# A graph layer on one core: GpSimd's gathers with a one-column memset once in three batches, and their wait for TensorE two batches further back

## The chip, the cores and the metric

The kernel runs on one core of a Trainium2 chip. A core has five engines with an instruction stream each: TensorE (PE: matmuls, PEld: its weight loads), VectorE (DVE), ScalarE (ACT), GpSimd (POOL) and SyncE (SP, which only issues DMAs). They wait for each other through semaphores. The metric is the device time of one execution in microseconds (us).

## The reference

One layer of a graph network with 12500 nodes of 160 features (64 scalars and 32 vectors of 3), and 400000 edges, sorted by their destination. Cut to what matters here (some lines joined):

```
h = jnp.maximum(_layernorm(x, axis=-1), 0.0)     # x0, x1: 64 scalars and 32 vectors of h; a = node_vec1
y0 = x0 @ W_l1_0 * a * inv0
y1 = jnp.einsum('nuc,uv->nvc', x1, W_l1_1) * a[:, :, None] * inv1
w = silu(edge_attr_16 @ fc_W1 * (1.0 / math.sqrt(FC_IN))) @ fc_W2 * (1.0 / math.sqrt(FC_H))   # 192: w_a, w_b, w_c, w_d
ys0, ys1 = y0[edge_src], y1[edge_src]
e0, e1 = edge_attr[:, :1], edge_attr[:, 1:]
mid0 = concatenate([w_a * ys0 * e0, w_d * einsum('euc,ec->eu', ys1, e1) * (1.0 / math.sqrt(3.0))])
mid1 = concatenate([(w_b * ys0)[:, :, None] * e1[:, None, :], (w_c * e0)[:, :, None] * ys1])
z0 = jnp.zeros((n, MID), mid0.dtype).at[edge_dst].add(mid0) * inv_nb
z1 = jnp.zeros((n, MID, 3), mid1.dtype).at[edge_dst].add(mid1) * inv_nb
out = x + C_S * (h's scalars @ W_sc0, vectors @ W_sc1) * a + C_X * (z0 @ W_l2_0, z1 @ W_l2_1) * a   # scaled
```

Each edge reads the row of y (y0 and y1 side by side, 160 wide) of a random node. This read is what GpSimd does in the kernel.

## The kernel before, in words

A first stage of about 190 us (the loop's first gather starts at 192.7) computes the node rows y and writes them to DRAM (y_d). The rest is one loop over the edges. They stand in 3125 tiles of 128, four tiles (GT) to a batch: 782 batches (NB). For each batch b:

- load(b): GpSimd gathers the rows of the 4 tiles into one buffer yg (128 x 4 x 160), with one indirect DMA for each tile (L579). There are 11 such buffers (YB). 24 of the 782 batches are not gathered but "made": their rows are rebuilt on the other engines, into buffers of their own (every 24 batches at first, 17 of them, then every 42).
- weigh(b): PE makes the 192 weights of each edge by 4 matmuls (L609) into one of two PSUM buffers pw; ScalarE then copies three of the edge's numbers beside them (L611). lift_rows(b): ScalarE scales the rows into yge (L521, four times).
- dots_of(b) and products(b): VectorE forms the products pr (L526 and L528; L532, L533, L536 and L537, by these lines in this order). L532 is the last to read yg. Once in three batches it also builds the selection matrices sel for 12 tiles (L628).
- sums(b): PE adds the products up by destination, pz += sel.T @ pr (L648).

The order of the instructions on PE, ScalarE and VectorE is that of the code in one loop over b, written by hand (`manual_schedule`); the engines run freely along it and are tied only by semaphores. An iteration b does weigh(b + 2), lift_rows(b + 2), dots_of(b + 1), products(b + 1), load(b + AHEAD), sums(b), and small steps for finished groups. As there are two pw, the weigh of b + 2 waits for the products of b; these wait for L526 and L528, which wait for L611 of their batch, which waits for PE's signal that the matmuls of weigh are done.

GpSimd is not in the list of hand-ordered engines. Its gathers wait for three things: for the DMA queue's semaphores (eight gathers back), at the first gather of a batch for the buffer, that is for L532 and L521 of the batch that had it 11 gathered batches before (DVE and Activation in the rows below), and, at one gather of each batch, for PE: `weighed[b]` holds the name of the last weigh matmul of batch b, and load(b) ties its gather k == 0 to `weighed[b - AHEAD + 2]`, with AHEAD = 10.

Of the kernel before, what the change touches and what calls it, by code (L numbers as in the profile page):

```python
# [9 lines left out]
F32 = mybir.dt.float32  # L10
# [7 lines left out]
P = 128  # L18
# [12 lines left out]
TG = 12  # L31
EG = 8
YB = 11
AHEAD = 10
WIDE = 3, 5
GN = 8
HN = 2
# [9 lines left out]
def kernel(  # L47
# [19 lines left out]
    nc = tc.nc  # L67
# [44 lines left out]
    def made(b):  # L112

        return made_at.index(b) if b in made_at else None
# [173 lines left out]
    def load_xe(blk):  # L288

        if blk not in blocks:  # L290
            xe = ld.tile([P, 512], F32, name="xe")
            v = e16[blk * P:(blk + 1) * P, :].rearrange("(s k f) (h c) -> k s (f h) c", s=4, k=2, h=2)
            for k in range(2):
                nc.sync.dma_start(xe[:, 256 * k:256 * (k + 1)], v[k])
            blocks[blk] = xe

    def e4_load(q):

        if q * EG < NU and q not in raws:
            lo, hi = q * EG * TG, min((q + 1) * EG * TG, TP)  # L300
            raw = ld.tile([P, EG * TG, 4], F32, name="raw")
            nc.sync.dma_start(raw[:, :hi - lo, :].rearrange("p t c -> p (t c)"), e4[:, lo * 4:hi * 4])
            raws[q] = raw
# [26 lines left out]
    engines = {mybir.EngineType.PE, mybir.EngineType.Activation, mybir.EngineType.DVE}  # L330
# [179 lines left out]
    keep = ctx.enter_context(tc.tile_pool(name="keep", bufs=1))  # L510
# [30 lines left out]
    with (  # L541
# [9 lines left out]
        leaving, weighed = [], {}  # L551
# [13 lines left out]
        def first_of(b):  # L565
            return min(b * GT if b <= short else short * GT + (T - short * GT) // 2 if b < NB else T, T)

        def tiles_of(b):
            return list(range(first_of(b), first_of(b + 1)))

        def load(b):
            r = made(b)
            if r is not None:
                rows[b] = xms[r]
                return
            yg = ygp.tile([P, GT, D], F32, name="yg")
            rows[b] = yg
            for k, t in enumerate(tiles_of(b)):
                ins = nc.gpsimd.indirect_dma_start(  # L579
                    out=yg[:, k, :], out_offset=None, in_=y_d,  # L580
                    in_offset=bass.IndirectOffsetOnAxis(ap=src_sb[:, t:t + 1], axis=0))
                if k == 0 and b - AHEAD + 2 in weighed:
                    tc.add_manual_dep(ins.ins, weighed[b - AHEAD + 2], mybir.DependencyInfo(
                        mybir.DependencyClass.Sync, mybir.DependencyReason.DATA), reason="no further ahead of the weights")

# [37 lines left out]
        def select(u, pw):  # L623

            n = min(TG, T - u * TG)
            sels[u] = selp.tile([P, TG, WN], F32, name="sel")
            for_each = pw[:, :, SP:].unsqueeze(1).to_broadcast([P, n, GT, WN // GT])
            nc.vector.tensor_tensor(sels[u][:, 0:n, :].rearrange("p t (k c) -> p t k c", k=GT), for_each,  # L628
                                    drel[:, u * TG:u * TG + n].unsqueeze(2).unsqueeze(3).to_broadcast(
                                        [P, n, GT, WN // GT]), ALU.is_equal)  # L630

        def dots_of(b):
            tmp = part.tile([P, GT, 3, M1], F32, name="tmp")
            dot(tmp, wts[b], rows[b], len(tiles_of(b)))
# [158 lines left out]
            for f in todo:  # L793
                f()

        order = tc.manual_schedule(engines={mybir.EngineType.PE, mybir.EngineType.Activation, mybir.EngineType.DVE})
        with order:
            e4_load(0)
            for blk in range(min(AHEAD - 1, NB - 1) * GT // BT + 1):
                load_xe(blk)  # L800
            for b in range(min(AHEAD - 1, NB)):
                load(b)
# [11 lines left out]
            dots_of(0)  # L814
            if AHEAD - 1 < NB:
                load(AHEAD - 1)
            select(0, wts[0])
# [3 lines left out]
            for g, e in enumerate(last_batch):  # L821
                at_end = e + 4 >= NB
                t = e + (1 if at_end else 2)
# [5 lines left out]
            for b in range(NB + 3):  # L829
                u, k = divmod(b, K)  # L830
# [22 lines left out]
                if b + AHEAD < NB:  # L853
                    load(b + AHEAD)
# [150 lines left out]
```

## Time and profile before

| | |
|---|---|
| median of 3 runs | 4750.52 us (4744.84 to 4751.22) |
| profiled execution | 4710.4 us, span 4708.5 us |
| mean granted TensorE clock | 0.916 |
| busy: PE, DVE, POOL, ACT | 85%, 75%, 63%, 37% of the span |
| the gather L579 | 3029 times, 949 ns each |

The profile is one execution, 40 us shorter than the median. In a group's row stand the busy time, the mean of one, and the idle time of the engine just before such an instruction with what ended it: "issue" is a gap in which the engine waited for nothing that the profile shows, and "remote" is a wait whose releaser the profile could not find on this core. In a row of the timeline stand the start, the duration, the engine, the line, the operation, how often it is repeated on end, and in brackets the idle time before it.

### The profile page before, as it was taken

The numbers are of one execution on the slowest core, as the hardware profiler recorded it, in microseconds if no ns is written. First come the engines' busy times: TensorE is split into PE (matmuls) and PEld (weight loads), VectorE is DVE, ScalarE is ACT, GpSimd is POOL, SyncE is SP. The second block draws the span as 40 slices with busy tenths as digits, with TensorE's granted clock in tenths as the row PEclk, the third lists the DMA queues.
The fourth block names the chain that finished last, engine by engine and source line by source line (L and its number), as shares of the span: only waits on it lengthen the run. The fifth ranks groups of instructions, "written<-read, shape, count | busy, mean of one in ns | idle before, by whom it ended". The sixth has DMA issues, their size and how long they took to land. (4 is left out here: it accounts for less than half of the span.)

```text
span 4708.5 us, 55993 instructions
## 1 busy us (share of the span) xinstructions
PE 4005.0 (85%) x16409; PEld 2323.1 (49%) x16409; DVE 3520.9 (75%) x6817; ACT 1764.2 (37%) x5610; POOL 2970.4 (63%) x3132
## 2 busy tenths in 40 slices
PE   4578888888888888888888888988888888888888
PEld 4444554444545554444444444555455455555554
DVE  4467777777777777777777777777777777777777
ACT  4333333333333333333333333333333333333333
POOL 5566666666666666666666666666666666666663
PEclk8689999999999999999999988999999999989899
DMA  7422222222222222222222222222222222232222
GB/s 215 122 62 63 67 65 68 68 61 66 65 69 66 66 67 65 63 65 68 67 65 66 65 64 62 66 67 62 68 62 66 62 68 62 68 107 64 63 63 58
DMA packets 228622, 335.20 MB, mean 71 GB/s; under 512 B 55098, under 2 KB 171910, under 8 KB 228054
## 3 DMA queue, kind: packets, MB, share of 16 engines
q0 software_dynamic: 150000, 256.20, 22.2%
q1 hardware_dynamic: 64642, 67.02, 4.6%
q10 hardware_dynamic: 13668, 8.36, 0.6%
q8 instruction: 130, 2.13, 0.2%
q14 instruction: 182, 1.49, 0.1%
HBM read 307.49 MB, written 23.88 MB: 70 GB/s over the span
## 5 line engine op out<-in xcount | busy, mean ns | idle before, releaser
L579 POOL DMA_INDIRECT yg<-y_d,src_sb x3029 | 2874.5, 949 | 1610.9 <-issue 711.1
L648 PE MATMUL pz<-pr,sel 128*128 128x384 f32 x6250 | 2488.7, 546 | 32.0 <-issue 16.3
L648 PEld LDWEIGHTS pz<-pr,sel 128*128 128x128 f32 x6250 | 1249.1, 210 | 979.0 <-issue 429.0
L609 PE MATMUL pw<-w,hT 64*128 64x192 f32 x6250 | 810.7, 366 | 553.4 <-issue 295.7
L611 ACT ACTIVATE pw<-raw 128x12 f32<-128x12 f32 (+1 forms) x782 | 140.4, 180 | 2812.0 <-remote 1339.0
L521 ACT ACTIVATE yge<-yg,raw 128x160 f32<-128x160 f32 x3029 | 1042.0, 422 | 0.3 <-DMA yg<-y_d,src_sb 0.3
L609 PEld LDWEIGHTS pw<-w,hT 64*128 64x128 f32 x6250 | 538.6, 195 | 944.7 <-issue 545.7
L526 DVE TENSOR_TENSOR tmp<-yg,pw 128x384 f32<-128x384 f32 (+1 forms) x758 | 416.6, 550 | 561.3 <-ACT pw L611 534.9
L533 DVE TENSOR_TENSOR pr<-pr,pw 128x768 f32<-128x768 f32 (+1 forms) x782 | 745.2, 953 | 27.0
L528 DVE TENSOR_REDUCE yg<-tmp 128x128 f32<-128x384 f32 (+1 forms) x758 | 450.3, 594 | 403.0 <-ACT yge L521 348.3
L628 DVE TENSOR_TENSOR sel<-pw,drel 128x1536 f32<-128x1536 f32 (+1 forms) x261 | 455.3, 1744 | 0.0
L592 PE MATMUL px<-xe,w 32*128 32x512 f32 x782 | 439.4, 643 | 11.1 <-issue 8.6
L532 DVE TENSOR_TENSOR pr<-pw,yg 128x384 f32<-128x384 f32 (+1 forms) x758 | 420.2, 554 | 17.8
L537 DVE TENSOR_TENSOR pr<-pw,yge 128x384 f32<-128x384 f32 (+1 forms) x782 | 428.3, 548 | 0.0
L536 DVE TENSOR_TENSOR pr<-pw,yge 128x256 f32<-128x256 f32 (+1 forms) x782 | 326.4, 417 | 0.0
L597 ACT ACTIVATE hT<-px 128x512 f32<-128x512 f32 x391 | 228.7, 585 | 12.4 <-issue 11.5
L592 PEld LDWEIGHTS px<-xe,w 32*128 32x128 f32 x782 | 114.7, 184 | 209.3 <-issue 142.9
L675 PEld LDWEIGHTS px<-wc,za 128*128 128x128 f32 x1110 | 151.3, 194 | 39.6 <-issue 7.6
L693 DVE SCALAR_TENSOR_TENSOR acc<-os,by,acc 128x160 f32 x370 | 144.2, 390 | 14.4 <-ACT os L680 1.1
L675 PE MATMUL px<-wc,za 128*128 128x96 f32 x1110 | 150.0, 272 | 0.8 <-ACT za L666 0.6
L376 POOL DMA_INDIRECT xr<-in_x,src_sb x88 | 87.2, 991 | 67.7 <-issue 27.8
L662 PEld LDWEIGHTS pz<-ident,zs 128*128 128x128 f32 x555 | 72.4, 141 | 58.1 <-issue 33.9
(126 smaller groups left out, 1683.1 us busy)
## 6 DMA issues: line engine op xcount, KB each, us to landing
yg<-y_d,src_sb POOLq DMA_INDIRECT x3029
xe<-in_e SPq DMA_DIRECT2D x196, 128.0 KB
xr_d<-xr SPq DMA_DIRECT2D x24, 320.5 KB
y_d<-ys ACTq DMA_DIRECT2D x12, 640.0 KB
xm<-xr_d SPq DMA_DIRECT2D x24, 320.0 KB
acc<-in_x SPq DMA_DIRECT2D x11, 640.0 KB
out<-acc SPq DMA_DIRECT2D x11, 640.0 KB
raw<-in_e SPq DMA_DIRECT2D x32, 192.0 KB
```

The lines of the kernel that those rows point to most:

```text
L521: nc.scalar.activation(yge[:, k, :], yg[:, k, :], AF.Copy, scale=e4v[:, k, 0:1])
L526: nc.vector.tensor_tensor(tmp[:, :n], y1, wt[:, :n, NW:NW + 3].unsqueeze(3).to_broadcast([P, n, 3, M1]), ALU.mult)
L528: nc.vector.tensor_reduce(yg[:, :n, M0:96], tmp[:, :n].rearrange("p t c u -> p t u c"), AX.X, ALU.add)
L532: nc.vector.tensor_mul(pr[:, :n, 0:96], wt[:, :n, 96:NW], yg[:, :n, 0:96])
L533: nc.vector.tensor_mul(pr[:, :n, 256:].rearrange("p t (c u) -> p t c u", c=3), pr[:, :n, 0:M0].unsqueeze(2).to_broadcast([P, n, 3, M0]), w ...
L536: nc.vector.tensor_mul(pr[:, :n, 96:160], wt[:, :n, 0:M0], yge[:, :n, 0:M0])
L537: nc.vector.tensor_mul(pr[:, :n, 160:256].rearrange("p t (c u) -> p t c u", c=3), wt[:, :n, M0:96].unsqueeze(2).to_broadcast([P, n, 3, M1] ...
L579: ins = nc.gpsimd.indirect_dma_start(out=yg[:, k, :], out_offset=None, in_=y_d, in_offset=bass.IndirectOffsetOnAxis(ap=src_sb[:, t:t + 1], ...
L592: nc.tensor.matmul(ph, w1[r, :], xe[r, :], start=True, stop=True)
L609: last = nc.tensor.matmul(pw[:, k, 0:NW], hids[s][r, o:o + P], w2[r, :], start=True, stop=True)
L628: nc.vector.tensor_tensor(sels[u][:, 0:n, :].rearrange("p t (k c) -> p t k c", k=GT), for_each, drel[:, u * TG:u * TG + n].unsqueeze(2).un ...
L648: nc.tensor.matmul(z_ps[g], sels[t // TG][:, t % TG, :], pr[:, k, M0:], start=first, stop=last)
```

## The change

Three edits. First, AHEAD goes from 10 to 12: load(b + 12) stands in iteration b, and the wait for PE in load(b) is for the weights of batch b - 10 instead of b - 8; it is tied to the last gather of the batch instead of k == 0. Second, once three batches have been passed since the last time, load(b) begins with a memset of one column of a small tile on GpSimd: 257 of them in all. Third, GpSimd joins the engines whose order is that of the code. The number of buffers stays 11.

```diff
-AHEAD = 10
+AHEAD = 12
+REST = 3
...
+        rest = keep.tile([P, 1], F32, name="rest")
+        rested = [0]
+
         def load(b):
             r = made(b)
+            rested[0] += 1
             if r is not None:
                 rows[b] = xms[r]
                 return
             yg = ygp.tile([P, GT, D], F32, name="yg")
             rows[b] = yg
-            for k, t in enumerate(tiles_of(b)):
+            if rested[0] >= REST and b >= AHEAD:
+                nc.gpsimd.memset(rest, 0.0)
+                rested[0] = 0
+            of = tiles_of(b)
+            for k, t in enumerate(of):
                 ins = nc.gpsimd.indirect_dma_start(
                     out=yg[:, k, :], out_offset=None, in_=y_d,
                     in_offset=bass.IndirectOffsetOnAxis(ap=src_sb[:, t:t + 1], axis=0))
-                if k == 0 and b - AHEAD + 2 in weighed:
+                if k == len(of) - 1 and b - AHEAD + 2 in weighed:
                     tc.add_manual_dep(ins.ins, weighed[b - AHEAD + 2], ...
...
-        order = tc.manual_schedule(engines={mybir.EngineType.PE, mybir.EngineType.Activation, mybir.EngineType.DVE})
+        order = tc.manual_schedule(engines={mybir.EngineType.PE, mybir.EngineType.Activation, mybir.EngineType.DVE,
+                                            mybir.EngineType.Pool})
```

GpSimd's instructions of before, from the middle of the program (each number behind yg is one batch's buffer; DMASW are the DMA queue's semaphores, PE the wait for weigh, DVE and Activation the wait for the buffer):

```order
1136 L579 DMA yg_11356<-y_d_60,src_sb_69 128x160 [waits DMASW3_49,PE_49]
1137 L579 DMA yg_11386<-y_d_60,src_sb_69 128x160 [waits DMASW4_49,DVE_49,Activation_49]
1138 L579 DMA yg_11386<-y_d_60,src_sb_69 128x160 [waits DMASW5_49]
1139 L579 DMA yg_11386<-y_d_60,src_sb_69 128x160 [waits DMASW6_49]
1140 L579 DMA yg_11386<-y_d_60,src_sb_69 128x160 [waits DMASW7_49,PE_49]
1141 L579 DMA yg_11425<-y_d_60,src_sb_69 128x160 [waits DMASW0_49,DVE_49,Activation_49]
```

The four gathers of yg_11386 stand with the buffer's wait on the first and PE's wait on the fourth: the scheduler has put k == 0 behind the other three.

The same after the change (L584 is the memset, L588 the gather; its Pool semaphore is that of the memset before):

```order
1182 L588 DMA yg_10995<-y_d_60,src_sb_69 128x160 [waits DMASW7_49,PE_49]
1183 L584 MEMSET rest_1704 128x1 [waits Pool_49]
1184 L588 DMA yg_11025<-y_d_60,src_sb_69 128x160 [waits DMASW0_49,DVE_49,Activation_49]
1185 L588 DMA yg_11025<-y_d_60,src_sb_69 128x160 [waits DMASW1_49]
1186 L588 DMA yg_11025<-y_d_60,src_sb_69 128x160 [waits DMASW2_49]
1187 L588 DMA yg_11025<-y_d_60,src_sb_69 128x160 [waits DMASW3_49,PE_49]
1188 L588 DMA yg_11065<-y_d_60,src_sb_69 128x160 [waits DMASW4_49,DVE_49,Activation_49]
```

The waits stand on the same places of a batch as before, buffer first and PE last; the value that PE's wait asks for is that of two batches earlier. New is the memset, which follows the last gather of one batch and stands ahead of the first of the next, as a rule once in 12 gathers. On PE, VectorE, ScalarE and SyncE the order is the same.

## The prediction

> **What bounds the kernel now.** I read the page's busy shares first, then the costliest groups, then the waits, and last a stretch of the timeline, because the first three leave open which engine makes the others late.
>
> ```profile
> PE 4005.0 (85%) x16409; PEld 2323.1 (49%) x16409; DVE 3520.9 (75%) x6817; ACT 1764.2 (37%) x5610; POOL 2970.4 (63%) x3132
> L579 POOL DMA_INDIRECT yg<-y_d,src_sb x3029 | 2874.5, 949 | 1610.9 <-issue 711.1
> L611 ACT ACTIVATE pw<-raw 128x12 f32<-128x12 f32 (+1 forms) x782 | 140.4, 180 | 2812.0 <-remote 1339.0
> L521 ACT ACTIVATE yge<-yg,raw 128x160 f32<-128x160 f32 x3029 | 1042.0, 422 | 0.3 <-DMA yg<-y_d,src_sb 0.3
> L526 DVE TENSOR_TENSOR tmp<-yg,pw 128x384 f32<-128x384 f32 (+1 forms) x758 | 416.6, 550 | 561.3 <-ACT pw L611 534.9
> ```
>
> TensorE (PE) has the largest share, but it is not full. Nobody waits for gathered rows: ScalarE lost 0.3 us to them in the whole run (third group). So Pool's gathers are not late. What is late is line 611, the small ScalarE copy that ends weigh: it starts when PE has reported its weigh matmuls, and VectorE's L526 starts behind it. There are 782 batches, and 758 of them are gathered, in 3029 gathers.
>
> ```profile
> ACT pw L611 <- remote: 1339.0, 196, 17.8
> ACT pw L611 <- PE pw L609: 712.1, 169, 9.3
> DVE tmp L526 <- ACT pw L611: 555.7, 236, 17.5
> POOL yg L579 <- issue: 711.1, 2304, 1.4
> POOL yg L579 <- remote: 449.8, 192, 4.0
> POOL yg L579 <- PE pw L609: 155.6, 75, 4.2
> ```
>
> The columns are total, times and longest, in us. Pool's own rests for a PE signal are the last two rows ("remote" is taken as the same wait with its releaser not found, for the stretch below shows the two alike): 192 + 75 = 267 rests, 449.8 + 155.6 = 605.4 us, 2.27 us each. One rest comes per 758 / 267 = 2.84 gathered batches. The other 2304 gaps are 0.31 us each (711.1 / 2304).
>
> ```profile
> 2053.49 0.95 POOL L579 DMA_INDIRECT yg<-y_d,src_sb  x1 [2.61 <-remote]
> 2058.33 0.92 PE L609 MATMUL pw<-w,hT 64*128 64x192 f32 x8 [1.44 <-DVE pr L537]
> 2059.35 0.18 ACT L611 ACTIVATE pw<-raw 128x12 f32<-128x12 f32 x1 [1.96 <-PE pw L609]
> ...
> 2062.93 0.92 PE L609 MATMUL pw<-w,hT 64*128 64x192 f32 x8
> ...
> 2067.27 0.94 POOL L579 DMA_INDIRECT yg<-y_d,src_sb  x1 [0.30 <-issue]
> ...
> 2070.68 0.18 ACT L611 ACTIVATE pw<-raw 128x12 f32<-128x12 f32 x1 [9.37 <-remote]
> 2070.87 0.94 POOL L579 DMA_INDIRECT yg<-y_d,src_sb  x1 [2.65 <-remote]
> 2070.90 0.55 DVE L526 TENSOR_TENSOR tmp<-yg,pw 128x384 f32<-128x384 f32 x1 [4.01 <-ACT pw L611]
> 2072.12 0.95 POOL L579 DMA_INDIRECT yg<-y_d,src_sb  x1 [0.30 <-ACT yge L521]
> 2073.47 0.56 DVE L532 TENSOR_TENSOR pr<-pw,yg 128x384 f32<-128x384 f32 x1
> ...
> 2079.68 0.95 POOL L579 DMA_INDIRECT yg<-y_d,src_sb  x1 [0.30 <-issue]
> 2080.69 0.92 PE L609 MATMUL pw<-w,hT 64*128 64x192 f32 x8
> 2082.49 0.18 ACT L611 ACTIVATE pw<-raw 128x12 f32<-128x12 f32 x1 [7.83 <-PE pw L609]
> 2082.68 0.95 POOL L579 DMA_INDIRECT yg<-y_d,src_sb  x1 [2.06 <-PE pw L609]
> 2083.93 0.95 POOL L579 DMA_INDIRECT yg<-y_d,src_sb  x1 [0.31 <-ACT yge L521]
> 2085.09 1.75 DVE L628 TENSOR_TENSOR sel<-pw,drel 128x1536 f32<-128x1536 f32 x1
> 2086.75 0.55 DVE L532 TENSOR_TENSOR pr<-pw,yg 128x384 f32<-128x384 f32 x1
> ```
>
> This is the core of the argument. A weigh that ends at 2058.33 + 0.92 = 2059.25, soon after a rest, is seen 0.10 us later (L611 at 2059.35). The next one ends at 2063.85, after eight gathers on end, and is seen only at 2070.68: 6.83 us late. It is seen when Pool has stopped: Pool's last gather before the rest ends at 2067.27 + 0.94 = 2068.21, the signal comes 2.47 us behind it, and Pool, which waits for the same signal, goes on 0.19 us after L611. At the next rest the last gather ends at 2080.63 and the signal comes 1.86 us behind it. Gathers start 1.25 us apart (0.95 + 0.30), so (2067.27 - 2053.49) / 1.25 makes 12 gathers in the first run and (2079.68 - 2070.87) / 1.25 makes 8 in the second. A pause of 1.86 us was needed after 8 gathers, of 2.47 us after 12: about 0.15 us per gather. I read this as a queue into which each gather puts slightly more than its 1.25 us clears; PE's signals stand behind it, and only a pause of Pool lets them out. The cause is inferred; the delay is in the rows.
>
> So the loop's clock is the rest. A cycle is 758 / 267 of a batch in 3029 / 267 = 11.3 gathers, 11.3 x 1.25 + 2.27 = 16.4 us. While PE waits for its own late signal the chain PE, ScalarE, VectorE, PE stands.
>
> **The change part by part.** The profiled execution took 4710.4 us (span 4708.5); the median of the runs is 4750.52, 40 us more. I sum on 4710 and add the 40.
>
> *The wait that moves to the last gather.* It stands last already in the order of before, so this place moves nothing: 0.
>
> *Ten batches back instead of eight.* Today the fourth gather of batch y + 8 waits for the weights of y; then it will be that of y + 10. By itself this only lets Pool start 8 gathers further ahead, once (8 x 1.25 = 10 us, not repeated). But right behind this gather stands the first gather of y + 11, which waits for its buffer: there are 11 buffers, so that is the one that products(y) reads, freed by L532 of batch y. Today the gather behind the rest is the first of y + 9, whose buffer was freed by y - 2 long ago; the rows show it at 2072.12 and 2083.93, 1.44 us after L611 both times, with the ordinary gap. After the change it must wait for L532(y): that ends at 2074.03 and at 2087.30, which is 3.35 and 4.81 us after L611 (the second time a select, L628, stands between), 4.08 on average. With the 0.19 us of a signal the gather starts 4.27 us after L611 instead of 1.44: 2.83 us more Pool time at each rest. Queued behind the waiting gather are all other gathers and nothing else; who waits for them is again nobody at once, but Pool's next stop, and so the next release of PE's signals, comes that much later.
>
> It does not apply always. The buffer goes back 12 batches instead of 11 when one of the last 11 batches was a made one, which takes no buffer. There are 782 - 758 = 24 of those, so 24 x 11 / 782 = 34% of the batches are spared. 267 x 0.66 = 176 rests x 2.83 = **+498 us**.
>
> Given back: in the second pause of 2.83 us Pool gathers nothing, so one gather less stands in the queue at the next rest (-0.15 x 176 = -26). And the longer pause leaves the next weigh prompt more often, so that a cycle holds a few per cent more batches: I take 5% fewer rests, 176 x 0.05 x (2.27 + 2.83) = -45. Neither is shown; from 0 to -200 for both is possible. With both: **+427**.
>
> *The memset.* There are 257 of them, 1 column each. The trace has no memset between gathers; the nearest rows are the constants at the start.
>
> ```profile
> 0.26 0.10 POOL L994 MEMSET const-float32-0.0<- 128x1 f32 x1 [0.26 <-issue]
> 0.28 0.10 POOL L994 MEMSET const-float32-1.0<- 128x1 f32 x1
> ```
>
> A second one starts 0.02 us behind the first and takes 0.10. So the price lies between 257 x 0.02 = 5 us and, if it waits for the gather's end and a full issue gap follows, 257 x (0.30 + 0.10) = 103 us. Such a pause counts against the one that the next rest needs, so of these I take about 0 on the path. On the other side it may let signals out early. The gap around it is at most 0.30 + 0.10 + 0.30 = 0.70 us, against 1.86 to 2.47 that the rests needed, some three tenths. If it released everything, the loop would come out near +70 (second rival below); three tenths of the way from 427 to 70 is **-107**. Ends: 0 and -357, and beyond it the first rival.
>
> The Trainium skill, in "GPSIMD Engine Reference", section 2.1 on instruction dispatch, says that consecutive Pool instructions are no barrier: completion holds back only who waits for the semaphore, not the next Pool instruction. The two memsets 0.02 us apart agree. By that rule the memset makes no pause at all, the -107 falls away, and the time would be some 5180; the rule speaks against the change, and I leave it as a reason for the upper end of the range.
>
> *The rest.* Nothing else moves on PE, VectorE, ScalarE or SyncE. Sum: 4710 + 498 - 26 - 45 - 107 = 5030, plus 40: **5070 us**, +6.7%. Its own range is 4880 to 5200: the give-backs at both ends, the memset releasing nothing (5180) or half of the way.
>
> **The rivals.** *The memset empties the queue (faster).* If the memset, though short, has to go through the same path as the gathers' writes, it is a drain: Pool goes on only when the queue is empty, and PE's signals come out with it every 12 gathers. Then a cycle of three batches is 12 x 1.25 = 15 us and a pause, with neither the rest for PE nor a wait for buffers, since the consumers are never far behind. With a pause of 1.0 us that is 16.0 / 3 = 5.33 us a batch against 16.4 / 2.84 = 5.77 now, -0.44 x 758 = -334; half of it where buffers still bind, -167, so about 4585. It decides from the point where the signal comes within about 1.5 us of the memset: beyond it the pause is as long as the rest it replaces (2.27). For it: nothing orders a memset against a gather's descriptors in this trace, so a drain isn't excluded. Against: the gap needed was 1.86 and more, and the constants' rows show no drain. 22%.
>
> *The memset lets signals out, but buffers still bind.* A release every 12 gathers without a rest, but the buffer wait stays: (15 + 0.4 + 2.83) / 3 = 6.08 us a batch in the 66%, (15 + 0.4) / 3 = 5.13 in the rest, against 5.77: 758 x (0.66 x 0.31 - 0.34 x 0.64) = -10, and with the second-order stalls of PE that I can't price up to +150; I take +70 on 4750: about 4820. 12%.
>
> *Nothing happens.* Pool's stops only move from one wait to another with the same number and length, for instance because L532 of y is done by the time that the fourth gather has gone (it would have to end 1.44 us after L611; the rows have 3.35 and 4.81). 4750. 6%.
>
> **How the numbers follow.** Forecast 60%, and the three rivals 22, 12 and 6. About 0.2% (10 us) is what a measurement of this kernel can tell from no change. Slower: 60 + 12 = 72%. Same: 6%. Faster: 22%. The range: the forecast's own, down through the second rival and no change, and to the middle of the first: 4580 to 5200. That leaves out half of the first rival and a tenth of the forecast, under 2 in 10.
>
> **What would show it.** Right: in the waits view Pool's gathers wait for VectorE's products (named L532 or what stands behind it, or "remote") in the order of 176 times with 2 to 4 us each, beside the rests for L609; L611's waits grow above 1339 + 712 us; the mean time from the first gather to the last grows from 5.77 to some 6.2 us a gathered batch; around most memsets the gap stays under 1 us and L611 does not start in it. Wrong: L611 starts within about 1 us of a memset in most cycles (then the rivals with release), the rests for PE vanish from the waits, or the gather behind a rest keeps starting 1.4 us after L611.

## The result, and the profile after

| | before | after |
|---|---|---|
| median of 4 runs on one chip | 4750.87 us (4744.84 to 4753.53) | 5054.58 us (5043.86 to 5069.26) |
| ratio, 95% interval | | 1.0643 [1.0614, 1.0672] |
| profiled execution, span | 4710.4, 4708.5 us | 5056.26, 5054.5 us |
| granted clock in it | 0.916 | 0.883 |

The change makes the kernel 303.7 us slower; 5070 had been forecast. The two profiles are not from one chip's level: before's 4710.4 us stand below all four of its runs in this table and at the level of the chips of the experiments (4707 to 4708 us). A profile of the changed kernel on such a chip (the last experiment) has a span of 5003.1 us, 294.6 more than before's; it is the like-for-like one and is given beside the other where it matters.

Lines have moved: before's L579, L521, L609, L611, L648 and L532 are L588, L522, L618, L620, L657 and L533 now. The groups of the page after:

```profile
PE 4151.4 (82%) x16409; PEld 2387.6 (47%) x16409; DVE 3517.3 (70%) x6817; ACT 1768.0 (35%) x5610; POOL 3008.6 (60%) x3389
L588 POOL DMA_INDIRECT yg<-y_d,src_sb x3029 | 2882.9, 952 | 1912.9 <-issue 882.8
L620 ACT ACTIVATE pw<-raw 128x12 f32<-128x12 f32 (+1 forms) x782 | 140.9, 180 | 3153.4 <-remote 1030.7
L522 ACT ACTIVATE yge<-yg,raw 128x160 f32<-128x160 f32 x3029 | 1041.9, 421 | 0.3 <-DMA yg<-y_d,src_sb 0.3
L527 DVE TENSOR_TENSOR tmp<-yg,pw 128x384 f32<-128x384 f32 (+1 forms) x758 | 416.1, 549 | 883.1 <-ACT pw L620 762.7
```

The same work takes the same busy time on VectorE and ScalarE (TensorE's grew by 146 us; see the clock under the twelfth buffer). What grew is idle time: 1610.9 to 1912.9 us in front of the gathers, 2812.0 to 3153.4 in front of the copy that ends weigh, 561.3 to 883.1 in front of VectorE's L527. Gathered rows are waited for as little as before (0.3 us). GpSimd's waits, after:

```profile
POOL yg L588 <- issue: 882.8, 2370, 4.7
POOL yg L588 <- remote: 377.8, 153, 9.0
POOL yg L588 <- ACT yge L522: 342.9, 204, 4.4
POOL yg L588 <- PE pw L618: 130.4, 64, 4.7
```

Two things are to be seen. The rests for TensorE became fewer: 153 + 64 = 217 and 508.2 us, where there were 267 and 605.4. And two kinds of gap that were of ordinary length before now hold long waits: "issue" goes to 4.7 us (1.4 before) and the gaps put down to ScalarE's L522 to 4.4 us. Before, these were

```profile
POOL yg L579 <- ACT yge L521: 83.6, 274, 0.3
```

The releaser's name misleads here; the timeline shows what these waits are:

```profile
2065.91 0.95 POOL L588 DMA_INDIRECT yg<-y_d,src_sb  x1 [0.30 <-issue]
...
2066.86 0.12 POOL L584 MEMSET rest<- 128x1 f32 x1
2067.17 0.95 POOL L588 DMA_INDIRECT yg<-y_d,src_sb  x1 [0.19 <-issue]
...
2069.67 0.94 POOL L588 DMA_INDIRECT yg<-y_d,src_sb  x1 [0.30 <-issue]
...
2073.66 0.18 ACT L620 ACTIVATE pw<-raw 128x12 f32<-128x12 f32 x1 [9.42 <-issue]
2073.85 0.94 POOL L588 DMA_INDIRECT yg<-y_d,src_sb  x1 [3.23 <-remote]
...
2077.91 0.55 DVE L533 TENSOR_TENSOR pr<-pw,yg 128x384 f32<-128x384 f32 x1
2079.20 0.95 POOL L588 DMA_INDIRECT yg<-y_d,src_sb  x1 [4.41 <-issue]
```

GpSimd rests 3.23 us for the weights and goes on at 2073.85, 0.19 us after L620. That is the fourth gather of a batch. The next one, the first gather of the next batch, waits again, 4.41 us, until L533 has read the buffer it needs (2077.91 + 0.55 = 2078.46) and 0.74 us more. This double stop is the change. The memset is in the same rows: it fills part of the gap, and the gathers around it stand 1.26 us apart, as all others do.

Sorted by the place of a gather in its batch, the time from the end of one gather to the start of the next is as follows (the first ten and the last two batches left out; where a memset stands in between, its 0.12 us are included):

| gap before the gather | before | after | after, another chip |
|---|---|---|---|
| first of a batch (buffer) | 227 us, none over 0.6 us | 711 us, 190 over 0.6 us, 2.83 us each | 710 us, 206 over 0.6 us, 2.63 us each |
| second and third | 461 us | 466 us | 466 us |
| fourth (weights) | 882 us, 315 over 0.6 us, 2.38 us each | 724 us, 226 over 0.6 us, 2.50 us each | 678 us, 213 over 0.6 us, 2.42 us each |

New waits at the first gather: +484 us. Less at the fourth: -158. With 8 us of longer gathers and 5 at the second and third this is the stream of gathers, 338 us longer (192.7 to 4652.8 us before, 193.7 to 4991.6 after); the span grew by 346. On the other chip it is +483 and -204, and the stream is 289 us longer. This is bookkeeping; that the first gather's wait is the cause is for the experiments.

### The profile page after: what moved, and what is told of

It reads as the page before. It is cut to its first block, busy times and chain, and to the rows that moved or that the text cites. A ratio compares the mean times of both kernels' runs of the same rounds, so it can differ in the third digit from the quotient of the medians.

```text
span 5054.5 us, 56248 instructions
## 1 busy us (share of the span) xinstructions
PE 4151.4 (82%) x16409; PEld 2387.6 (47%) x16409; DVE 3517.3 (70%) x6817; ACT 1768.0 (35%) x5610; POOL 3008.6 (60%) x3389
## 5 line engine op out<-in xcount | busy, mean ns | idle before, releaser
L588 POOL DMA_INDIRECT yg<-y_d,src_sb x3029 | 2882.9, 952 | 1912.9 <-issue 882.8
L657 PE MATMUL pz<-pr,sel 128*128 128x384 f32 x6250 | 2560.1, 557 | 107.0 <-ACT za L675 57.1
L657 PEld LDWEIGHTS pz<-pr,sel 128*128 128x128 f32 x6250 | 1275.3, 215 | 1111.0 <-issue 544.2
L618 PE MATMUL pw<-w,hT 64*128 64x192 f32 x6250 | 869.7, 374 | 630.8 <-issue 331.9
L620 ACT ACTIVATE pw<-raw 128x12 f32<-128x12 f32 (+1 forms) x782 | 140.9, 180 | 3153.4 <-remote 1030.7
L618 PEld LDWEIGHTS pw<-w,hT 64*128 64x128 f32 x6250 | 569.1, 200 | 1037.6 <-issue 596.1
L522 ACT ACTIVATE yge<-yg,raw 128x160 f32<-128x160 f32 x3029 | 1041.9, 421 | 0.3 <-DMA yg<-y_d,src_sb 0.3
L527 DVE TENSOR_TENSOR tmp<-yg,pw 128x384 f32<-128x384 f32 (+1 forms) x758 | 416.1, 549 | 883.1 <-ACT pw L620 762.7
L533 DVE TENSOR_TENSOR pr<-pw,yg 128x384 f32<-128x384 f32 (+1 forms) x758 | 419.9, 554 | 17.8
```

The costliest lines, as they stand in the source:

```text
L522: nc.scalar.activation(yge[:, k, :], yg[:, k, :], AF.Copy, scale=e4v[:, k, 0:1])
L527: nc.vector.tensor_tensor(tmp[:, :n], y1, wt[:, :n, NW:NW + 3].unsqueeze(3).to_broadcast([P, n, 3, M1]), ALU.mult)
L533: nc.vector.tensor_mul(pr[:, :n, 0:96], wt[:, :n, 96:NW], yg[:, :n, 0:96])
L588: ins = nc.gpsimd.indirect_dma_start(out=yg[:, k, :], out_offset=None, in_=y_d, in_offset=bass.IndirectOffsetOnAxis(ap=src_sb[:, t:t + 1], ...
L618: last = nc.tensor.matmul(pw[:, k, 0:NW], hids[s][r, o:o + P], w2[r, :], start=True, stop=True)
L657: nc.tensor.matmul(z_ps[g], sels[t // TG][:, t % TG, :], pr[:, k, M0:], start=first, stop=last)
```

## Experiments

The runs went to several chips, so each is compared with the kernel before on its own chip (4708 us for the first eight, 3967 for the three after them, 4707 for the last). Times in an expectation are, where it says nothing else, for a kernel before of 4750 us; by the ratio, 5050 there is about 5005 here.

**Without the memsets** (theory: they cost and bring nothing).

```
-REST = 3
+REST = 10**9
```

> The changed kernel without any of its 257 memsets in the loop; all else as changed. Buffer theory (the cost is the first gather of batch y + 11, which waits for L533 of batch y right behind the wait for the weights of y): 5050 us, as with the memsets, because the gap around a memset is 0.31 us like any other. Memset theory (the memset delays the gathers or upsets them): back near 4750 us. Release theory (the memset lets some signals of TensorE out early and the cost would be worse without it): about 5160 us.

5007.4 us against 4707.9: 1.0631 [1.0613, 1.0649]. The memsets are worth nothing in either direction; memset theory and release theory fall.

**Memsets alone** (AHEAD back at 10).

```
-AHEAD = 12
+AHEAD = 10
```

> The changed kernel with AHEAD back at 10: memsets and hand-ordered GpSimd stay, the wait for the weights is eight batches back again. Buffer theory: 4750 us, no wait of GpSimd for L533. Memset theory: near 5050 us. Release theory: below 4700 us.

4709.7 us: 1.0005 [0.9995, 1.0015]. Nor do the memsets, GpSimd's hand order and the place of the wait do anything without the two batches.

**One batch further back instead of two** (AHEAD = 11).

> The changed kernel with AHEAD = 11: the wait for the weights is nine batches back, the buffers stay 11. Behind the rest stands then the first gather of y + 10, which needs the buffer of y - 1, free long before. Buffer theory: a step, so still near 4750 us (4700 to 4800). Depth theory (running further ahead of the weights costs by itself, gradually): half of the way, about 4900 us.

4715.8 us: 1.0014 [1.0004, 1.0023]. A step, not a slope: nine batches back cost 0.1%, ten cost 6.3%. GpSimd's waits have the shape of before, with no long "issue" gap and L522's at 0.3:

```profile
POOL yg L588 <- issue: 714.7, 2354, 1.9
POOL yg L588 <- remote: 379.2, 167, 6.6
POOL yg L588 <- PE pw L618: 236.4, 98, 5.0
POOL yg L588 <- ACT yge L522: 63.1, 241, 0.3
```

**The same with one buffer less** (AHEAD = 11, YB = 10).

```
-AHEAD = 12
+AHEAD = 11
-YB = 11
+YB = 10
```

> AHEAD = 11 and one buffer less, 10: the wait for the weights of y is followed at once by the wait for the buffer that products(y) reads, as in the changed kernel, with the look-ahead one batch shorter. Buffer theory: near 5050 us (5030 to 5100), with some 190 waits of 2.8 us at the first gather of a batch. Depth theory: as the run with AHEAD = 11 and 11 buffers, about 4900 us or whatever that shows.

5006.6 us: 1.0639 [1.0612, 1.0665], the loss of the change at a look-ahead one shorter. 192 waits over 0.6 us stand at first gathers, 2.81 us each.

```profile
POOL yg L588 <- issue: 895.2, 2360, 6.5
POOL yg L588 <- remote: 342.3, 139, 4.0
POOL yg L588 <- ACT yge L522: 323.4, 197, 4.3
POOL yg L588 <- PE pw L618: 127.4, 60, 4.0
```

**A twelfth buffer** (AHEAD = 12).

```
-YB = 11
+YB = 12
-        tc.tile_pool(name="nrx", bufs=10) as nrx,
+        tc.tile_pool(name="nrx", bufs=9) as nrx,
-                pm = mk.tile([P, D + NT], F32, name="m_p")
+                pm = mk.tile([P, D + NT], F32, name="m_p", bufs=1)
```

> The changed kernel with a twelfth buffer (room made for it: one buffer less in the node stage's gathers of x, 9 instead of 10, and one instead of two for a tile of the made batches). The gather behind the rest, the first of y + 11, then needs the buffer of y - 1. Buffer theory: near 4710 us (before's level on this chip, +-40), no wait at the first gather of a batch. Depth theory: 5010 us or more, as AHEAD is still 12.

4725.1 us: 1.0037 [1.0023, 1.0051]. With all of the change in place, one buffer takes back 6.3% to 0.4%; its first gather starts at 197.6 us, where before's starts at 192.7, which is some 5 of the 17 us that remain; from there to the last gather's end it takes 4459.8 us, before 4460.1. None of its first gathers waits over 0.6 us, and the long gaps are gone from "issue" and L522:

```profile
POOL yg L588 <- issue: 702.9, 2336, 1.4
POOL yg L588 <- ACT yge L522: 75.3, 264, 0.3
```

These five runs settle it: what counts is the distance between the two waits. Depth theory falls with this run and with the two at AHEAD = 11, which differ by one buffer alone.

The granted clock goes with the loss: 0.880 to 0.890 in all runs with the double stop (the changed kernel, without memsets, with one buffer less), 0.915 to 0.925 in those with memsets alone, at AHEAD = 11 and with the twelfth buffer. How much of the loss passes through the lower clock, and whether it is more than a consequence of the stops, was not separated.

**A rest that lasts.**

```
-                nc.gpsimd.memset(rest, 0.0)
+                for _ in range(6):
+                    nc.gpsimd.memset(rest, 0.0)        # rest is 480 columns wide
```

> The changed kernel (AHEAD = 12, 11 buffers) with a rest that really lasts: six memsets of 480 columns instead of one of 1 column, about 2.5 to 3 us, once in three batches. Queue theory: the signals come out in this rest, 12 gathers having asked for about 2.4 us, so the rests for TensorE largely go; the buffers are then waited for less; (15 + 3) / 3 = 6.0 us a batch, 4800 to 4900 us, faster than the changed kernel though GpSimd does more. Theory that a memset is no rest at all for the signals: 758 / 3 x 3 = 760 us on top of the changed kernel, 5700 us or more.

4963.8 us: 1.0542 [1.0522, 1.0562]. The direction is that of the queue theory: GpSimd works 773 us more and the kernel is still faster than the changed one (1.0631 to 1.0643), because the rests for TensorE go from 217 to 45, 74.8 us, and the waits over 0.6 us at first gathers, the memsets not counted, from 190 to 10.

```profile
L585 POOL MEMSET rest<- 128x480 f32 x1542 | 772.6, 501 | 74.2
POOL yg L589 <- remote: 41.0, 20, 5.5
POOL yg L589 <- PE pw L619: 33.8, 25, 2.4
```

The size was missed by 64 us: six memsets take 3.30 us on end, more than the 2.5 to 3 assumed. The signals do come out in the planned stop: of 243 copies that an idle ScalarE starts over 1.5 us behind their weigh, 198 start while these memsets run. That the rests became fewer may also be due to the slower stream, 1.55 us a gather on average; the run at 1.56 us below has few rests too.

**Pacing every gather** (AHEAD = 10; a memset of the columns named ahead of each gather instead of one in three batches).

```
             for k, t in enumerate(of):
+                if b >= AHEAD:
+                    nc.gpsimd.memset(rest, 0.0)        # rest is 240, 400, 80 or 160 columns wide
                 ins = nc.gpsimd.indirect_dma_start(
```

> AHEAD = 10, and a memset of 240 columns ahead of every gather instead of one of 1 column in three batches: some 0.30 us of memset in each gap, gathers about 1.44 us apart instead of 1.25. Queue theory (each gather adds about 0.15 us more to the queue ahead of TensorE's signals than its 1.25 us clears): from 1.40 us on nothing is held, the copy of line 620 starts within about 0.3 us of the weigh's end in nearly all batches, and GpSimd hardly rests; 4 x 1.44 = 5.76 us a batch, 4600 to 4720 us. Stop theory (TensorE's signals need one stop of about 2 us, however the gathers are spaced): the rests stay as long and the pacing comes on top, 758 x 4 x 0.19 = 576 us, so 5200 us or more.

4712.7 us: 1.0013 [1.0003, 1.0023].

```profile
L586 POOL MEMSET rest<- 128x240 f32 x2989 | 940.9, 315 | 2.0
POOL yg L587 <- remote: 51.9, 54, 4.0
POOL yg L587 <- PE pw L617: 45.6, 49, 2.5
L619 ACT ACTIVATE pw<-raw 128x12 f32<-128x12 f32 (+1 forms) x782 | 141.9, 181 | 2796.3 <-issue 1371.7
```

With gathers 1.43 us apart GpSimd hardly rests (103 times, 97.5 us), as the queue theory has it, and the time does not rise, against the stop theory's 5200. But the signals are not free. Counted batch by batch, from the end of the weigh's last matmul or of ScalarE's work before the copy, whichever is later, the copy still starts over 1.5 us late in 274 batches (319 in before), 1467 us in all batches together (1463 in before). In 128 of the 274 a gather is running at that moment, so a stop is not the only thing that lets a signal out. GpSimd only no longer runs into the limit. So the queue theory is wrong in its number at least: 1.40 us between gathers is no threshold. And the rests are not what sets the time: most of them went, the late signals stayed, and so did the time.

> As the run with 240 columns, with 400: about 0.43 us of memset, gathers about 1.6 us apart. Queue theory: signals prompt everywhere, the kernel bound by GpSimd at 6.4 us a batch, about 5050 us. Stop theory: rests on top of 6.4 us a batch, over 5500 us.

A single execution: 4977.0 us. At 1.56 us between gathers the signals are prompt: by the same count 4 batches are over 1.5 us. (The copy starts over 1.5 us behind its weigh in 161, but in nearly all of them ScalarE was still at the batch before.) Now ScalarE waits for rows:

```profile
L522 ACT ACTIVATE yge<-yg,raw 128x160 f32<-128x160 f32 x3029 | 1246.7, 426 | 2328.8 <-DMA yg<-y_d,src_sb 2318.7
```

This is what the queue theory expected, at 6.28 us a batch instead of 6.4. So the signals are late in 274 batches at 1.43 us and in 4 at 1.56; whether the spacing does it, or that the other engines now wait for GpSimd, these two runs do not tell. On such a chip pacing ties at 1.43 us and loses at 1.56; narrower spacings were not run there.

> As the run with 240 columns (AHEAD = 10, a memset ahead of every gather), with 80 columns: about 0.18 us of memset, gathers some 1.30 us apart. Queue theory: each gather leaves about 0.10 us more than its time clears, so the rests shrink less than the pacing adds or about as much: between 307 and 124 rests over 1 us, shorter than 2.4 us each, 4650 to 4710 us. Stop theory: 3029 x 0.05 = 140 us on top, 4850 us.

4145.2 us against 3966.7 for the kernel before on the same chip: 1.0450 [1.0433, 1.0468].

> The same with 160 columns: gathers some 1.36 us apart. Queue theory: rests shorter and fewer again, between the runs with 80 and 240 columns; as both ends (1.25 and 1.43 us) give 4710, the best place may lie between: 4620 to 4700 us. If the trade is one to one everywhere: 4710 us.

4347.8 us: 1.0958 [1.0940, 1.0977].

> 160 columns and AHEAD = 11, the deepest look-ahead at which the gather behind the rest does not need the buffer of the batch just released. Queue theory: a signal that is held for a short time no longer stops GpSimd at once, so equal to the run with 160 columns and AHEAD = 10 or up to 40 us faster. Buffer theory: no wait at the first gather of a batch, as with AHEAD = 11 before; if such waits appear, 5000 us.

4347.6 us: 1.0959 [1.0941, 1.0977]. This one has AHEAD = 11; it equals the run with 160 columns and has no wait over 0.6 us at a first gather, as both theories allowed, but there was little to be tested: all three runs are far off the times expected, for the chip was another kind. There the kernel before takes 3967 us, 16% less than on the others, at a granted clock of 0.98 against 0.92. The waits of the run with 80 columns show why:

```profile
ACT yge L522 <- DMA yg<-y_d,src_sb: 1126.1, 1292, 5.0
ACT pw L619 <- PE pw L617: 793.3, 482, 6.6
...
POOL yg L587 <- issue: 475.5, 2720, 2.0
...
POOL yg L587 <- PE pw L617: 7.7, 24, 2.0
```

TensorE's signals come at once (677 batches within 0.3 us, 14 over 1.5, and none of these with ScalarE idle), GpSimd does not rest for them, and the kernel is bound by the stream of gathers. No profile of the kernel before was taken there; by this reading 3029 gathers at about 1.25 us are 3790 of its 3967 us. There each hundredth of a microsecond of pacing is paid in full (80 to 160 columns: 1.363 - 1.296 = 0.067 us x 2989 = 200; measured 202.6).

**The changed kernel once more.**

> The changed kernel as it is, once more, beside the kernel before. On a chip where the kernel before takes some 3967 us (as in the last three runs: TensorE's signals are not held there and GpSimd does not rest for them), hold theory: the buffer wait falls away with the hold, 3967 us, within 0.3% of before. If the buffer wait or the look-ahead costs by itself: some 4100 us or more. On a chip where the kernel before takes some 4710 to 4750 us: 1.064 times before again, about 5010 to 5055 us.

It came to a chip of the first kind: 5005.6 us against 4707.1, 1.0631 [1.0613, 1.0649], the same loss, with the same waits (last column of the table above). What the change does on a chip like that of 3967 us was not run and stays open.

No version measured beats the kernel before.

## Why the prediction was right, step by step

- *The place of the wait moves nothing*: right, the run with memsets alone is at 1.0005.
- *The new wait, 176 rests x 2.83 us = +498*: the mechanism is shown by the step between AHEAD = 11 and 12, by the run with one buffer less and by the twelfth buffer. Measured: 190 such waits of 2.83 us with the ordinary gap in them, 2.53 us more each, +484. The number was too low and the price too high, and they met. (The 267 rests from which the number comes are those that the waits view puts down to PE or "remote"; by place, before has 315 over 0.6 us at the fourth gather.) Only 125 of the 190 stand directly behind a rest for the weights, as the prediction had it for all of them; the other 65 stand alone. And GpSimd goes on 0.74 us after L533, not the 0.19 us taken from the rest for the weights.
- *Who pays for it: the next release of TensorE's signals comes later*: borne out. From the end of a weigh to its copy 2.43 us pass on average in before, 3.26 after and 3.14 on the other chip; 3.15 to 3.17 without the memsets and with one buffer less, but 2.36 to 2.55 with memsets alone, at AHEAD = 11 and with the twelfth buffer. From one weigh to the second next it is 11.41 us in before and 12.13 after on the other chip (batches 24 to 775), and 0.67 of the 0.72 more stand between weigh and copy.
- *The loop's clock is the rest*: too strong. In the run with 240 columns 605 us of rests went down to 98 and the time stayed; what stayed with it is the late signals.
- *Given back, -26 and -45*: mis-sized. The gaps at the fourth gather fell by 158 us (204 on the other chip, which is the like-for-like one): 226 stops over 0.6 us for 315, 28% fewer where 5% was taken, presumably because the wait for a buffer is itself a stop of GpSimd and lets signals out, as in the planned rest of 3.30 us; this was not tested by itself.
- *The memset, -107*: wrong by all of it. This was the term taken three tenths of the way to a full release. It lies in the issue gap, costs 118 ns off the path, lets nothing out, and its removal changes nothing. The Trainium skill's rule in "GPSIMD Engine Reference", section 2.1, that consecutive Pool instructions are no barrier between GpSimd's cores and that completion does not hold back the next one, agrees with 1.26 us between the gathers around it, and the prediction should have gone by it. What a memset takes, 118 ns here, the rule does not say. That the sum came out in spite of this error is luck: it and the one before have opposite signs, -158 to -204 us measured for both, against -26 - 45 - 107 = -178.
- *The rivals*: an emptied queue, signals let out and no effect at all are ruled out by the ratio, and the first two also by the run without memsets.
- *What would show it*: the waits came in the number and length named, but under the names "issue" and L522, not under a product of VectorE. L620's idle time grew as said, 2812.0 to 3153.4 us. Around 209 of the 257 memsets the gap stays under 1 us. A gathered batch takes (4991.6 - 193.7) / 758 = 6.33 us and took (4652.8 - 192.7) / 758 = 5.88, where the prediction had 6.2 and 5.77: both too low by about 0.1, the step right.
- *Not asked*: that the late signals are a trait of some chips. The price of 6% is a price on these.

## What to carry to other kernels

When a producer is held back by two waits, one for a signal and one for a free buffer, count in batches how far apart they stand: a limit that is loosened until it meets the next one does not remove a stop, it adds the second wait to the first. Before an instruction is used as a pause, look for whether it fits in a gap that is there anyway, as one column did here. And a wait that is put down to "issue" or to a harmless neighbour, yet is longer than such gaps are elsewhere, is read by the place of the instruction in its order and by what its buffer needs.

## What the runs showed of the hardware

- TensorE's signals to ScalarE and GpSimd come up to several microseconds late while GpSimd issues gathers on end, on most of the chips used and not on one: an idle ScalarE starts the copy over 1.5 us late in 319 of 782 batches in before's profile, in none in the three paced runs on the other chip. In 298 of the 319 GpSimd stands still at that moment. The same kernel takes 4707 to 4751 us and 3967 us. Why the chips differ is open, and so is the cause of the hold: neither a queue that is clear from 1.40 us between gathers on nor a fixed stop fits the run at 1.43 us, which has 274 late signals and no longer time.
- A GpSimd memset took 118 ns for 1 column, 181 for 80, 249 for 160, 315 for 240, 448 for 400: about 115 ns and 0.83 ns a column, of which up to 0.14 us hides in the 0.3 us between two gathers (80 columns: 1.296 us from gather to gather, 1.254 without).
- A gather that waits for VectorE starts 0.74 us after the product's end (in 188 of 190 such waits after the change), one that waits for TensorE 0.19 us after ScalarE sees the same signal.
